# One transfer for both image halves, stores by column half, an earlier branch, and a projection that writes PSUM in image order

## The chip, the cores and the metric

The kernel runs on 1 core of one Trainium2 chip. The metric is device time in microseconds of that core. Everything is float32. TensorE (PE) multiplies and writes PSUM, VectorE (DVE) and ScalarE (ACT) read PSUM and SBUF, GpSimd (POOL) works on SBUF and issues transfers, SyncE (SP) only issues transfers. Transfers issued by SP and ACT go through the hardware queues, those issued by POOL through the software queue; all of them are carried out by the core's 16 DMA engines.

## What is computed

The input is one image x of 48 channels and 256x256 pixels. Two layers follow one another:

```
# layer 0
qkv = einsum('bchw,oc->bohw', gn(x), w_qkv)            # 144 channels
qkv = depthwise 3x3 convolution of qkv
q, k, v = heads(unfold 4x4 patches, 8 heads)           # 96 values x 64*64 patches (+ a border) per head
attn = softmax(l2norm(q)^T l2norm(k) * temperature)    # 4096 x 4096 per head
x = x + einsum('bchw,oc->bohw', fold(v attn), w_proj)
# layer 1, on windows of 64x64
x = x + sum over t of 3: einsum('bcphqw,twW,thH,tcC->bCpHqW', gn(x), Ws, Hs, Cs)
```

`gn` is a group normalisation over 16 groups of 3 channels, so each layer begins only when the statistics of its whole input are known.

## The kernel before

The image's 256 rows are kept as two halves of 128 rows: channel c of half s lies on partition 16 + 48 s + c, so that 96 partitions are filled. `rows_of[s]` names the 48 partitions of half s. `both_halves` and `both_parts` return a list with one piece of DRAM for each half, and every caller loops over that list and issues one transfer of 48 partitions for each half.

The stages, in order of time:

1. **Load and statistics** (L427 to L445). x is read into `xr` (112 partitions, 128 rows of 256) in ten parts, two transfers each, all on SP's queue. DVE takes `bn_stats` of each part as it arrives; then `group_stats` gives mean and deviation and everything that follows on PE depends on it.
2. **1x1 convolution of the first two heads** (L491 to L519). Sixteen steps. In each, PE multiplies into PSUM, ACT and DVE move the result to one of four tiles `oi`, and four transfers (column half `c` times image half `s`, half of them on SP, half on POOL) store it to `t1[0]` in DRAM. The `oi` tiles are in the same pool as `xr`.
3. **Depthwise convolution of head 0** (`depthwise_first`). Ten rows of patches: `Depthwise.load` reads `pad` from `t1` in three transfers, the taps run on PE (matrices `diag`, made on POOL at L387) or on DVE, and three stores write queries, keys and values to `qkv[0]`.
4. **A branch** (L538). If the temperatures are large, another path computes row maxima. With these inputs it is not taken, but every engine loads the flag, compares and passes a series of semaphore events.
5. **Attention** (L572 to L801), one head after the other, in an order written out by hand (`tc.manual_schedule`). Sixteen steps g per head. The depthwise convolution of head h+1 runs beside head h. During head 0 also the 1x1 convolution of heads 2 to 7 runs, in 32 `Strip`s: `load` reads 4 rows of both halves into one of two tiles `xs` (two transfers on SP), `run` multiplies, `store` writes to `t1[1]` (two transfers on SP). On SP's queue the load of strip j+2 stands behind the store of strip j. During head 7 the rows of x for three parts of the projection are loaded into `xts` (L799).
6. **Projection** (`project`, L809 to L902). The image is cut into 8 parts of 32 rows, 16 in each half. For each, PE multiplies the attention's output (`pot0` or `pot`, in patch order) by `w_proj`, DVE adds the result to x in place and takes the statistics for layer 1, and POOL stores the rows to `x1s`. For parts 3 to 7 the rows of x are loaded on SP's queue at L894, behind the loads of `pot`. PSUM holds a patch order (kj, py, px), and DVE reads and writes with a step of four elements when it adds.
7. **Layer 1** (L930 to L1083). Pieces of x1 in SBUF and rows read back from `x1s` go through three products; the output is stored from POOL.

The lines of the projection and of the strip load that matter:

```
for half, rows in enumerate(both_parts(x1s, k, part * R, R)):          # L829
    nc.gpsimd.dma_start(out=rows, in_=xt[rows_of[half]])
for s, rows in enumerate(both_parts(xc, k, part * R, R)):              # L893
    nc.sync.dma_start(out=xt[rows_of[s]], in_=rows)
```

Of the kernel before, what the change touches and what calls it, by code (L numbers as in the profile page):

```python
# [19 lines left out]
HALF = H // 2  # L20
# [29 lines left out]
def conv_preact_kernel(  # L50
# [73 lines left out]
    for z in range(3):  # L124
        for j in range(CH):
            p = (z * CH + j) * 6
            nc.gpsimd.dma_start(out=dwt[p : p + 6], in_=dws[z])
    nmx = const.tile([128, NH * NT // 128], F32, name="nmx")
    nc.vector.memset(nmx, 0.0)
# [34 lines left out]

    def both_halves(t, y, n, base=0):

        return [t[:, base + s * HALF + y : base + s * HALF + y + n, :] for s in range(2)]

    order = [(3, 0), (3, 1), (2, 0), (2, 1), (1, 1), (1, 0), (0, 1), (0, 0)]

    def both_parts(t, k, y, n):

        yw, i = order[k]
        y += yw * WS + i * TP // PX * KS
        return [t[:, y + s * (WS // 2) : y + s * (WS // 2) + n, :] for s in range(2)]

    class Strip:
# [5 lines left out]
        def load(self):  # L183
            self.xs = xss[self.j % len(xss)]
            for s, rows in enumerate(both_halves(xc, SR * self.j, SR)):
                nc.sync.dma_start(out=self.xs[rows_of[s]], in_=rows)

# [20 lines left out]
        def store(self):  # L208
            for s, rows in enumerate(both_halves(t1[1], SR * self.j, SR, base=1)):
                nc.sync.dma_start(out=rows, in_=self.ot[:, s])  # L210
# [171 lines left out]
    def depthwise_first():  # L382

        with tc.tile_pool(name="dg", bufs=1) as dg, tc.tile_pool(name="dps", bufs=3, space=PSUM) as dps:
            diag = dg.tile([NP1, 9, NP1], F32, name="diag")
            for t in range(9):
                nc.gpsimd.tensor_scalar_mul(diag[:, t, :], ident[:NP1, :NP1], dwt[:, 0, t : t + 1])  # L387
# [3 lines left out]
            def taps(r):  # L391
# [12 lines left out]
            with tc.manual_schedule(engines={mybir.EngineType.PE}):  # L404
                taps(0)
                for i in range(0, CR + 1, 2):
                    if i + 1 not in on_tensor:
                        taps(i + 1)
                    taps(min(i + 2, CR))
                    for d in rows[i + 6 : i + 8]:  # L410
# [15 lines left out]

    with tc.tile_pool(name="xn", bufs=1) as xnp, tc.tile_pool(name="cst", bufs=1) as cst, tc.tile_pool(  # L427
        name="nps", bufs=2, space=PSUM
    ) as nps, tc.tile_pool(name="pw", bufs=3, space=PSUM) as pw:
# [8 lines left out]
        for i, LR in enumerate(parts):  # L438
            j = sum(parts[:i])
            clear(xr[:, j : j + LR, :])  # L440
            for s, rows in enumerate(both_halves(xc, j, LR)):
                nc.sync.dma_start(out=xr[rows_of[s], j : j + LR, :], in_=rows)
            for i in range(0, LR, 2):
                nc.vector.bn_stats(st0[:, (j + i) // 2, :], xr[:, j + i : j + i + 2, :].rearrange("p a b -> p (a b)"))
# [47 lines left out]
        QR = HALF // 2  # L492
        ois = [xnp.tile([128, 2, OR, W + 2], F32, name=f"oi{i}") for i in range(4)]
        for t in ois:
            nc.gpsimd.memset(t[:, :, :, 0:1], 0.0)
            nc.gpsimd.memset(t[:, :, :, W + 1 : W + 2], 0.0)
        for n in range(QR // OR):
# [19 lines left out]
            for c in range(2):  # L517
                for s, rows in enumerate(both_halves(t1[0], c * QR + n * OR, OR, base=1)):
                    (nc.gpsimd if s else nc.sync).dma_start(out=rows, in_=ot[c * 64 : c * 64 + M0, s])  # L519

# [13 lines left out]
    for t in xss:  # L534
        nc.gpsimd.memset(t[:OFF], 0.0)
    depthwise_first()

    with tc.If(nc.values_load(large) > 0):  # L538
        with tc.tile_pool(name="sps", bufs=2, space=PSUM) as sps:
            for j in range(HALF // SR):  # L540
# [3 lines left out]
                w.store()  # L544
        for h in range(1, NH):
            depthwise_all(h)
        with tc.tile_pool(name="mk", bufs=NM) as mk, tc.tile_pool(name="mq", bufs=2) as mq, tc.tile_pool(
            name="mps", bufs=2, space=PSUM
        ) as mps:
            for h in range(NH):  # L550
# [5 lines left out]
                for nb in range(NB):  # L556
# [12 lines left out]
                    b = h * NB + nb  # L569
                    nc.vector.tensor_reduce(nmx[:, b : b + 1], mx, AX.X, ALU.max, negate=True)  # L570

    with tc.tile_pool(name="ahead", bufs=2) as ah, tc.tile_pool(name="ae", bufs=3) as ae, tc.tile_pool(  # L572
# [128 lines left out]
        with tc.manual_schedule():  # L701
            load_query(0, 1)
            block = scores(0, 0)
            for h in range(NH):
                more = h + 1 < NH
                rows = {r: Depthwise(h + 1, r) for r in range(CR + 1)} if more else {}
                for g in range(NG):
# [68 lines left out]
                    for k in range(NK):  # L776
# [18 lines left out]
                        if not more and 0 < g <= 2 * NX and k in (1, 3):  # L795
                            i = (g - 1) * 2 + k // 2
                            t, y = i // 4, i % 4 * (RP // 4)
                            for half, src in enumerate(both_parts(xc, t, y, RP // 4)):
                                nc.sync.dma_start(out=xts[t][rows_of[half], y : y + RP // 4, :], in_=src)  # L799
                        if not more and 2 * NX < g <= 2 * NX + KS and k in (1, 3):  # L800
# [8 lines left out]
        def project(k, pot, part, xt, new):  # L809

            R = xt.shape[1]
            n = R // KS * PX
            xv = xt.rearrange("p (py ki) (px kj) -> p ki kj py px", ki=KS, kj=KS)
            for ki in range(KS):
                ps = new(n)
                step = 512 // n
                for i in range(0, KS, step):
                    nc.tensor.matmul(  # L818
                        ps[:, i : i + step, :],
                        lhsT=wp,  # L820
                        rhs=pot(ki)[:PF, i : i + step, part * n : (part + 1) * n],
                        start=True,
                        stop=True,
                    )
                nc.vector.tensor_add(xv[:, ki], ps.rearrange("p k (py px) -> p k py px", py=R // KS), xv[:, ki])
            for i in range(0, R, 2):
                nc.vector.bn_stats(st1[:, len(seen), :], xt[:, i : i + 2, :].rearrange("p a b -> p (a b)"))
                seen.append(i)
            for half, rows in enumerate(both_parts(x1s, k, part * R, R)):  # L829
                nc.gpsimd.dma_start(out=rows, in_=xt[rows_of[half]])  # L830

        def in_big(n):

            ps = big.tile([128, 2, 512], F32, name="big")
            return ps[:PF].rearrange("p a (b n) -> p (a b) n", n=n)

# [24 lines left out]

    with tc.tile_pool(name="pj", bufs=1) as pj, tc.tile_pool(name="pjs", bufs=1) as pjs, tc.tile_pool(
        name="pps", bufs=3, space=PSUM
    ) as pps, tc.tile_pool(name="pp1", bufs=1, space=PSUM) as pp1:
# [21 lines left out]
        for k, xus_k in enumerate(xus, 1):  # L886
# [3 lines left out]
            if k >= NX:  # L890
                for part, xt in enumerate(xus_k):
                    R = xt.shape[1]
                    for s, rows in enumerate(both_parts(xc, k, part * R, R)):  # L893
                        nc.sync.dma_start(out=xt[rows_of[s]], in_=rows)  # L894
            for part, xt in enumerate(xus_k):
# [4 lines left out]
                    xt,  # L900
                    lambda n: pps.tile([PF, KS, n], F32, name="pps"),
                )  # L902
# [222 lines left out]
```

## Time and profile before

| what | value |
|---|---|
| median of 3 runs | 3569.47 us (3565.06 to 3577.12) |
| the profiled execution | 3563.74 us, its span 3561.9 us |
| mean granted TensorE clock | 0.978 |
| PE busy | 3324.8 us, 93% of the span |
| DVE, ACT, POOL busy | 1982.3, 1953.2, 588.0 us |
| HBM read, written | 230.82 MB, 144.90 MB |

The span runs from the first to the last instruction; the profiled execution's own time is 1.8 us longer. By stage, read from the order of the instructions: x is loaded and its statistics taken until 88 us; the first 1x1 convolution runs to 150 us; the depthwise convolution of head 0 from 158 to 277 us; the first product of the attention begins at 291 us; head 0 lasts to about 745 us and the attention to 3188 us; the projection begins at 3196 us, layer 1 at 3325 us. A share of busy time is an average over stages that have different limits, so each stage must be looked at by itself.

### The profile page before, as it was taken

The page shows a single profiled execution, that of the slowest core. Times are in us where ns is not written, and L with a number is a line of the kernel's source. Part 1 is how long each engine was busy: PE and PEld are TensorE (multiplying, and loading weights), DVE is VectorE, ACT ScalarE, POOL GpSimd, SP SyncE. Part 2 cuts the span into 40 slices and gives each one's busy share as a digit, 9 for nine tenths or more (in the row PEclk, how much of TensorE's full clock was granted, in tenths as well). Part 3 has the DMA queues.
Part 4 walks back from the last instruction along what each step waited for, and adds up shares of the span by engine and source line. Part 5 has one row for each costly group of instructions (what it writes and reads, how often), then busy time and mean ns, then how long its engine had stood idle before and what let it go on. Part 6 is the DMA issues. An engine that isn't in the chain of part 4 may idle for free.

```text
span 3561.9 us, 63455 instructions
## 1 busy us (share of the span) xinstructions
PE 3324.8 (93%) x25964; PEld 1856.3 (52%) x25964; DVE 1982.3 (56%) x2965; ACT 1953.2 (55%) x2891; POOL 588.0 (17%) x658
## 2 busy tenths in 40 slices
PE   0696999999999999999999999999999999986898
PEld 0243445555555555555555555555555555542576
DVE  4372666148825882588258826872687222228544
ACT  3234667657755665566557655764666444423243
POOL 2231111012211220122012201220122010000123
PEclk9897999999999999999999999999999999997999
DMA  9445666543332333333333332333333222109764
GB/s 147 143 127 147 164 161 165 168 137 93 86 87 79 93 87 83 89 95 82 85 87 95 79 87 83 93 89 78 87 96 93 76 53 51 33 25 295 176 163 112
DMA packets 232563, 380.22 MB, mean 107 GB/s; under 512 B 77858, under 2 KB 176546, under 8 KB 229192
## 3 DMA queue, kind: packets, MB, share of 16 engines
q1 hardware_dynamic: 192246, 262.98, 27.6%
q0 software_dynamic: 36544, 110.12, 13.7%
q8 instruction: 208, 3.41, 0.4%
q10 hardware_dynamic: 3474, 2.97, 0.3%
q14 instruction: 91, 0.75, 0.1%
HBM read 230.82 MB, written 144.90 MB: 105 GB/s over the span
## 4 chain that ended last, share of the span: by engine, by line
PE 85%; DMA 5%; DVE 1%; issue 1%; SPq 0%; ACT 0%; POOL 0%; POOLq 0%; DVEq 0%; ACTq 0%
PE big L361 39%; PE big L651 36%; PE pb L1015 2%; PE pa L991 2%; PE pc L1034 2%; DMA lxq<-in_x_dram 2%; PE big L194 2%; DMA xs<-in_x_dram 2%; PE pst L599 1%; DMA kt<-qkv 0%; PE pn L268 0%; PE pps L818 0%; DVE acc L249 0%; PE big L818 0%; DMA pad<-t 0%
## 5 line engine op out<-in xcount | busy, mean ns | idle before, releaser
L617 ACT ACTIVATE e<-big,nmx 128x1024 f32<-128x1024 f32 x1024 | 1144.6, 1118 | 909.6 <-PE big L361 883.7
L361 PE MATMUL big<-kt,qt 128*128 128x512 f32 x6144 | 1459.9, 395 | 29.7 <-DMA qt<-qkv 23.4
L651 PE MATMUL big<-e,vn 128*32 128x512 f32 x12288 | 1348.4, 593 | 1.0 <-DVE vn L635 1.0
L361 PEld LDWEIGHTS big<-kt,qt 128*128 128x128 f32 x6144 | 1143.3, 189 | 370.0 <-issue 122.0
L665 DVE TENSOR_TENSOR oacc<-big,oacc 128x1024 f32<-128x1024 f32 x359 | 438.5, 1221 | 766.9 <-PE big L651 766.9
L651 PEld LDWEIGHTS big<-e,vn 128*32 128x32 f32 x12288 | 384.5, 110 | 881.9 <-issue 815.5
L249 DVE SCALAR_TENSOR_TENSOR acc<-pad,dwt,acc 126x1024 f32<-126x1024 f32 x592 | 765.5, 1293 | 34.0 <-ACT acc L230 18.3
L319 POOL DMA_DIRECT2D qkv<-o x72 | 52.9, 734 | 1341.0 <-ACT o L303 1341.0
L313 POOL TENSOR_TENSOR ol<-o,oh 126x1024 fp32r<-126x1024 f32 x78 | 185.3, 2376 | 266.5 <-DVE ss L264 197.4
L631 DVE TENSOR_REDUCE zt<-zs 128x1 f32<-128x5 f32 x256 | 38.6, 151 | 327.6 <-ACT e L617 291.2
L617 ACT ACTIVATION_READ_ACCUMULATOR e<-big,nmx 128x1 f32 x1024 | 195.8, 191 | 0.0
L303 ACT COPY o<-acc 126x1024 f32<-126x1024 f32 x74 | 161.8, 2186 | 0.0
L1022 ACT COPY lyt<-pb 128x1024 f32<-128x1024 f32 x69 | 69.9, 1012 | 111.6 <-PE pb L1015 111.6
L201 ACT ACTIVATE ot<-big,bias 108x1024 f32<-108x1024 f32 x64 | 68.0, 1112 | 112.2 <-PE big L194 74.9
L230 ACT ACTIVATE acc<-pad,dwt 126x1024 f32<-126x1024 f32 x74 | 84.1, 1136 | 77.8 <-DMA pad<-t 69.7
L676 POOL DMA_DIRECT2D os__70<-oacc x86 | 50.3, 593 | 424.2 <-DVE oacc L665 414.4
L238 PE MATMUL dps<-pad,diag 126*126 126x512 f32 x216 | 95.6, 602 | 19.3 <-DMA pad<-t 19.3
L260 ACT ACTIVATE sq<-acc 126x1024 f32<-126x1024 f32 x74 | 78.2, 1057 | 59.6 <-DVE acc L249 48.5
L335 POOL DMA_DIRECT2D kt<-qkv x44 | 22.9, 538 | 516.6 <-PE big L361 418.9
L818 PE MATMUL pps<-pot,wp 112*112 112x512 f32 x112 | 68.9, 775 | 39.0 <-DMA pot<-os__70 20.7
L1001 DVE COPY lzt<-pa 128x864 f32<-128x864 f32 (+1 forms) x69 | 67.5, 1000 | 59.9 <-PE pa L991 59.9
L264 DVE TENSOR_REDUCE ss<-sq 126x64 f32<-126x1024 f32 x80 | 97.3, 1218 | 5.4 <-ACT sq L260 5.3
(154 smaller groups left out, 1973.4 us busy)
## 6 DMA issues: line engine op xcount, KB each, us to landing
pad<-t SPq DMA_DIRECT2D x238, 254.0 KB
t<-ot SPq DMA_DIRECT2D x64, 435.4 KB
qkv<-ol POOLq DMA_DIRECT2D x78, 336.0 KB, 6.4
qkv<-oh POOLq DMA_DIRECT2D x70, 336.0 KB, 5.7
qt<-qkv SPq DMA_DIRECT2D x176, 96.0 KB
xs<-in_x_dram SPq DMA_DIRECT2D x64, 192.0 KB
out_dram<-lrt POOLq DMA_DIRECT2D x96, 128.0 KB, 3.5
qkv<-o POOLq DMA_DIRECT2D x72, 168.0 KB, 3.4
```

What stands on the lines that cost most here:

```text
L194: nc.tensor.matmul(ps[:M1, s, :], lhsT=wr[r], rhs=self.xs[r, i : i + 2, :].rearrange("p a b -> p (a b)"), start=True, stop=True,)
L230: nc.scalar.mul(self.acc, self.pad[:, 0:KS, 0:W], dwt[:, self.h, 0:1])
L238: nc.tensor.matmul(ps[:, i, :], lhsT=diag[:, tap, :], rhs=self.pad[:, y : y + 2, dx : dx + W], start=(tap == 0), stop=(tap == 8),)
L249: nc.vector.scalar_tensor_tensor(self.acc, self.pad[:, dy : dy + KS, dx : dx + W], dwt[:, self.h, tap : tap + 1], self.acc, ALU.mult, ALU.add,
L260: nc.scalar.activation(self.sq, self.acc, AF.Square)
L264: nc.vector.tensor_reduce(self.ss, self.sq.rearrange("p a (x b) -> p x a b", b=KS), AX.XY, ALU.add)
L303: nc.scalar.copy(self.o.rearrange("p (a b) x -> p a b x", a=KS), self.acc.rearrange("p a (x b) -> p a b x", b=KS))
L313: eng.tensor_sub(self.ol, self.o, self.oh.bitcast(F32))
L361: nc.tensor.matmul(ps[:, i, :], lhsT=qt[:, r, q0 : q0 + 128], rhs=kts[2 * j + i][:, r // 2, :], start=(r == 0), stop=(r == 2),)
L617: nc.scalar.activation(e[:, j * 1024 : (j + 1) * 1024], ps.rearrange("p a b -> p (a b)"), AF.Exp, bias=nmx[:, b : b + 1], accum_out=zs[:, ...
L651: nc.tensor.matmul(ps[p * 32 : (p + 1) * 32, u, :], lhsT=vn[:, c * 32 : (c + 1) * 32], rhs=e[:, n * 512 : (n + 1) * 512], start=(i == 0), ...
L665: nc.vector.tensor_add(oaccs[h, pair], ps, old)
```

## The change

- `both_halves` and `both_parts` return one view whose first dimension is the half (`s c y x`) instead of a list of two views. Six callers that looped over the halves now issue one transfer of 96 partitions: the load of `xr`, `Strip.load`, the loads of `xts` and of the projection's rows of x, and the store to `x1s`. `Strip.store` loops over the view's first dimension and issues two transfers as before.
- The first convolution stores by column half: one transfer for both image halves, `c` outermost, column half 0 from SP and 1 from POOL. The `oi` tiles are five, in a pool of their own.
- `diag` is made at the start of the kernel, in a pool of its own.
- The branch stands in front of `depthwise_first`; the path that is not taken computes head 0's convolution too.
- The projection's PSUM tiles have image order: PE writes them with a step of four elements, DVE reads and writes contiguous rows. `pxts` has a pool of its own.

```
@@ L125
+    taps = ExitStack()
+    diag = taps.enter_context(tc.tile_pool(name="diag", bufs=1)).tile([NP1, 9, NP1], F32, name="diag")
+    for t in range(9):
+        nc.gpsimd.tensor_scalar_mul(diag[:, t, :], ident[:NP1, :NP1], dwt[:, 0, t : t + 1])
@@ L165
-        return [t[:, base + s * HALF + y : base + s * HALF + y + n, :] for s in range(2)]
+        return t[:, : 2 * HALF, :].rearrange("c (s y) x -> s c y x", s=2)[:, :, y : y + n, :]
@@ L171
-        y += yw * WS + i * TP // PX * KS
-        return [t[:, y + s * (WS // 2) : y + s * (WS // 2) + n, :] for s in range(2)]
+        y += i * TP // PX * KS
+        return t.rearrange("c (w s y) x -> w s c y x", s=2, y=WS // 2)[yw, :, :, y : y + n, :]
@@ L183 Strip.load
-            for s, rows in enumerate(both_halves(xc, SR * self.j, SR)):
-                nc.sync.dma_start(out=self.xs[rows_of[s]], in_=rows)
+            nc.sync.dma_start(out=self.xs[OFF:], in_=both_halves(xc, SR * self.j, SR))
@@ L438
-            for s, rows in enumerate(both_halves(xc, j, LR)):
-                nc.sync.dma_start(out=xr[rows_of[s], j : j + LR, :], in_=rows)
+            nc.sync.dma_start(out=xr[OFF:, j : j + LR, :], in_=both_halves(xc, j, LR))
@@ L490
-        ois = [xnp.tile([128, 2, OR, W + 2], F32, name=f"oi{i}") for i in range(4)]
+        ois = [oip.tile([128, 2, OR, W + 2], F32, name=f"oi{i}") for i in range(5)]
@@ L517
-                for s, rows in enumerate(both_halves(t1[0], c * QR + n * OR, OR, base=1)):
-                    (nc.gpsimd if s else nc.sync).dma_start(out=rows, in_=ot[c * 64 : c * 64 + M0, s])
+                (nc.gpsimd if c else nc.sync).dma_start(
+                    out=both_halves(t1[0][:, 1:, :], c * QR + n * OR, OR).rearrange("s c y x -> c s y x"),
+                    in_=ot[c * 64 : c * 64 + M0],
+                )
@@ L536
-    depthwise_first()
-
     with tc.If(nc.values_load(large) > 0):
...
-        for h in range(1, NH):
+        for h in range(NH):
             depthwise_all(h)
...
+    depthwise_first()
+    taps.close()
@@ L798
-                            for half, src in enumerate(both_parts(xc, t, y, RP // 4)):
-                                nc.sync.dma_start(out=xts[t][rows_of[half], y : y + RP // 4, :], in_=src)
+                            nc.sync.dma_start(
+                                out=xts[t][OFF:, y : y + RP // 4, :], in_=both_parts(xc, t, y, RP // 4)
+                            )
@@ L809 project
-            n = R // KS * PX
-            xv = xt.rearrange("p (py ki) (px kj) -> p ki kj py px", ki=KS, kj=KS)
+            PY = R // KS
+            xv = xt.rearrange("p (py ki) x -> p ki py x", ki=KS)
             for ki in range(KS):
-                ps = new(n)
-                step = 512 // n
-                for i in range(0, KS, step):
+                ps = new(PY)
+                for y in range(0, PY, 2):
                     nc.tensor.matmul(
-                        ps[:, i : i + step, :],
+                        ps[:, y : y + 2, :].rearrange("p py (px kj) -> p kj py px", kj=KS),
                         lhsT=wp,
-                        rhs=pot(ki)[:PF, i : i + step, part * n : (part + 1) * n],
+                        rhs=pot(ki)[:PF, :, (part * PY + y) * PX : (part * PY + y + 2) * PX],
                         start=True,
                         stop=True,
                     )
-                nc.vector.tensor_add(xv[:, ki], ps.rearrange("p k (py px) -> p k py px", py=R // KS), xv[:, ki])
+                nc.vector.tensor_add(xv[:, ki], ps, xv[:, ki])
...
-            for half, rows in enumerate(both_parts(x1s, k, part * R, R)):
-                nc.gpsimd.dma_start(out=rows, in_=xt[rows_of[half]])
+            nc.gpsimd.dma_start(out=both_parts(x1s, k, part * R, R), in_=xt[OFF:])
@@ L866
-        pxts = [pj.tile([PF, r, W], F32, name=f"pxt{t}") for t, r in enumerate((RP, RP, PR))]
+        pxts = [pjx.tile([PF, r, W], F32, name=f"pxt{t}") for t, r in enumerate((RP, RP, PR))]
@@ L893
-                    for s, rows in enumerate(both_parts(xc, k, part * R, R)):
-                        nc.sync.dma_start(out=xt[rows_of[s]], in_=rows)
+                    nc.sync.dma_start(out=xt[OFF:], in_=both_parts(xc, k, part * R, R))
```

More of the change, by code (lines that the diff above doesn't have):

```diff
@@ L162, in group_stats, with both_halves @@
         nc.vector.reciprocal(rstd, g)
-    def both_halves(t, y, n, base=0):
-        return [t[:, base + s * HALF + y : base + s * HALF + y + n, :] for s in range(2)]
+    def both_halves(t, y, n):
+        return t[:, : 2 * HALF, :].rearrange("c (s y) x -> s c y x", s=2)[:, :, y : y + n, :]
     order = [(3, 0), (3, 1), (2, 0), (2, 1), (1, 1), (1, 0), (0, 1), (0, 0)]
@@ L208, in store @@
         def store(self):
-            for s, rows in enumerate(both_halves(t1[1], SR * self.j, SR, base=1)):
+            for s, rows in enumerate(both_halves(t1[1][:, 1:, :], SR * self.j, SR)):
                 nc.sync.dma_start(out=rows, in_=self.ot[:, s])
@@ L384, in depthwise_first, with on_row @@
         with tc.tile_pool(name="dg", bufs=1) as dg, tc.tile_pool(name="dps", bufs=3, space=PSUM) as dps:
-            diag = dg.tile([NP1, 9, NP1], F32, name="diag")
-            for t in range(9):
-                nc.gpsimd.tensor_scalar_mul(diag[:, t, :], ident[:NP1, :NP1], dwt[:, 0, t : t + 1])
             rows = [Depthwise(0, r, dg) for r in range(CR + 1)]
             on_tensor = [r for r in range(CR + 1) if r % 2 == 0 or r == CR]
-            def taps(r):
+            def on_row(r):
                 if r in on_tensor:
@@ L404, in depthwise_first @@
             with tc.manual_schedule(engines={mybir.EngineType.PE}):
-                taps(0)
+                on_row(0)
                 for i in range(0, CR + 1, 2):
                     if i + 1 not in on_tensor:
-                        taps(i + 1)
-                    taps(min(i + 2, CR))
+                        on_row(i + 1)
+                    on_row(min(i + 2, CR))
                     for d in rows[i + 6 : i + 8]:
@@ L427, in conv_preact_kernel @@
     with tc.tile_pool(name="xn", bufs=1) as xnp, tc.tile_pool(name="cst", bufs=1) as cst, tc.tile_pool(
+        name="oip", bufs=1
+    ) as oip, tc.tile_pool(
         name="nps", bufs=2, space=PSUM
@@ L828, in project @@
                 seen.append(i)
-            for half, rows in enumerate(both_parts(x1s, k, part * R, R)):
-                nc.gpsimd.dma_start(out=rows, in_=xt[rows_of[half]])
+            nc.gpsimd.dma_start(out=both_parts(x1s, k, part * R, R), in_=xt[OFF:])
         def in_big(n):
             ps = big.tile([128, 2, 512], F32, name="big")
-            return ps[:PF].rearrange("p a (b n) -> p (a b) n", n=n)
+            return ps[:PF].rearrange("p a (b x) -> p (a b) x", x=W)
         with tc.manual_schedule():
@@ L860, in load_piece @@
         eng.dma_start(out=piece(yw, i)[rows_of[s], y : y + n, :], in_=x1s[:, y0 : y0 + n, :])
-    with tc.tile_pool(name="pj", bufs=1) as pj, tc.tile_pool(name="pjs", bufs=1) as pjs, tc.tile_pool(
+    with tc.tile_pool(name="pjx", bufs=1) as pjx, tc.tile_pool(name="pj", bufs=1) as pj, tc.tile_pool(name="pjs", bufs=1) as pjs, tc.tile_pool(
         name="pps", bufs=3, space=PSUM
@@ L900, in conv_preact_kernel @@
                     xt,
-                    lambda n: pps.tile([PF, KS, n], F32, name="pps"),
+                    lambda n: pps.tile([PF, n, W], F32, name="pps"),
                 )
```

## The prediction

> **What bounds the kernel now.** I read first the page's chain of work that ended last, then the busy time by stretches, then the branch's line. The whole is PE's:
>
> ```profile
> span 3561.9 us, 63455 instructions
> PE 85%; DMA 5%; DVE 1%; issue 1%; SPq 0%; ACT 0%; POOL 0%; POOLq 0%; DVEq 0%; ACTq 0%
> ```
>
> The change touches none of the two attention products that make up most of PE's share. It touches transfers, and three stages that wait for them. Busy time by stretch (columns: stretch, length, busy time of PE, PEld, DVE, ACT, POOL, granted clock, DMA share, GB/s):
>
> ```profile
> 0.00:88.00 88.00, 0.00 (x0) 0.00 (x0) 41.97 (x89) 30.89 (x12) 23.32 (x54) 1.00 0.97 148
> ...
> 170.00:175.00 5.00, 5.00 (x12) 2.06 (x11) 3.11 (x3) 1.15 (x1) 0.00 (x0) 0.96 0.45 170
> 190.00:195.00 5.00, 5.00 (x13) 2.16 (x12) 4.86 (x5) 0.00 (x0) 0.00 (x0) 1.00 0.45 178
> 345.00:745.00 400.00, 389.84 (x2440) 202.41 (x2440) 212.08 (x329) 263.29 (x373) 57.19 (x52) 0.98 0.62 167
> 3210.00:3310.00 100.00, 67.19 (x110) 24.08 (x110) 82.99 (x87) 23.81 (x6) 7.51 (x15) 0.77 1.00 290
> ```
>
> The load of x (first line) has all 16 DMA engines busy and no PE. Head 0 (fourth) has PE at 97% and DMA at 62%. The projection (last) has the DMA engines full again. Lines two and three are the key: only `pad` loads run there, at a share of 0.45, which is 7.2 of 16 engines, however many wait behind. The `pad` view in DRAM has a first dimension of 7, while 42 partitions stand on the other side.
>
> The branch, by its source line on SP:
>
> ```profile
> L538 SPq EVENT_SEMAPHORE  x8: 17/17/17, 285.1 to 285.7; - x8
> L538 SPq TENSOR_LOAD <-large x1: 982/982/982, 281.2 to 281.2; - x1
> L538 SPq COMPARE_BRANCH  x1: 50/50/50, 282.2 to 282.2; - x1
> ```
>
> SP reaches it last, after head 0's stores; its first attention load is issued at 286.3, and POOL and ACT wait for SP's events.
>
> **What the Trainium skill says.** "DMA: Bandwidth & Descriptors", section "Why a DMA increments its semaphore by 16 and not by 1": a transfer runs on the largest k up to 16 that divides the slowest dimension of both sides, as the instruction carries it. The 7 busy engines of `pad` (7 against 42) agree. The same section says that hardware-queue transfers take the lowest-numbered k engines, software-queue ones k consecutive engines that rotate; no line here shows either. "PSUM — Partial Sum Buffer", "Specifications (TRN2)": a non-contiguous pattern slows matmuls significantly, with no figure; all matmuls of before write contiguously, so the trace is silent.
>
> **The change part by part.** The new view is (s=2, c=48, y, x) against 96 partitions. The largest divisor of both 2 and 96 is 2: **each merged transfer runs on two engines.** One engine moves 170/7 to 178/7 GB/s in the `pad` lines, 24.3 to 25.4; I take 25, so a pair moves 50 GB/s.
>
> *Load of x.* 2 x 48 x 128 KB = 12.58 MB, by 50 GB/s 252 us, and the first packet some 2 us after the start: 254 us, against about 88 x 0.97 = 85 us and a last `bn_stats` at 88. Nothing hides it, since everything waits for the statistics. **+165** (155 to 175 from 25.4 and 24.3 GB/s, less a microsecond or two). The ten DMA issues saved on SP (0.31 us each) are hidden. `diag`, nine POOL instructions of 0.6 us, moves from 160 us to behind the `dwt` loads at 81 us; the load covers it, and without that cover it costs its 5.3 us. On POOL only the `zr` memset and the zero rows' stores stand behind it.
>
> *First convolution.* 36 channels stay outermost and 12 divides 36, so the engines stay as they were. 64 stores become 32 of twice the size, and a fifth buffer eases ACT's 21.6 us and DVE's 13.8 us of waits for `t<-oi`. The traffic, 64 x 145 KB = 9.3 MB over 12 x 25 GB/s, needs 31 us of the 50 us that the stores take, so at most some 15 us could go; bigger transfers could also hold a buffer longer. **-5** (-12 to +3).
>
> *The branch.* Moved ahead, it stands between the last `t1[0]` stores and the `pad` loads of SP and ACT. SP needs 281.2 to 286.3, 5.1 us, for it; now it waits there from 153.6 to 158.35, 4.7 us, for the stores to land, which covers the new place to within half a microsecond. POOL's memsets and DVE's next work wait for the same stores. Without that cover it costs 5 us. At the old place 5.1 us go, but the key loads then wait for head 0's last stores, issued until 281.1 and landing after a POOL-like median of 6.4 us. The first query and strip loads, needing older rows only, can be early; PE's idle time from 269.3 to 291.2 is the limit. **-5** (-15 to +4).
>
> *Head 0's strips.* 32 loads of 393 KB, 15.7 us per pair at a whole-step pace of two per 26.4 us. Over the 400 us line, an average engine is busy 0.62 x 400 = 248 us. Without the strips' 11.4 MB (28 us per engine) 220 are left. The two lowest engines carry more: 7.0 MB of `pad` on 7 engines is 40 us instead of 17; 26 MB of `t<-ot` on 12 (108 channels) is 87 instead of 65. That gives 265 us, and with strips on two engines, 11.4 MB/50 = 228, **493 us in a stretch of 400**. If bytes alone count (167 GB/s, so 167 us instead of 248), it is 412. So DMA takes over from PE as the bound of head 0: +12 to +93 at perfect overlap, more if SP's queue stalls behind the pair. I take **+90** (10 to 190). `Strip.store` is unchanged; 32 saved issues are hidden. *Head 7's* 12 merged loads (7.9 us each, two per 22 us) can delay query loads: **+2** (0 to 6).
>
> *Projection.* x for parts 3 to 7 is 7.86 MB: 157 us on the pair, from SP's first issue at 3207. In the same queue stand five `pot` loads, a sixteenth of 1.57 MB per engine each, 5 x 3.9 = 20 us; one rotating x1s store of 1.57 MB on the same pair would add some 20. The last x lands between 3384 and 3404; now it lands at 3302.9. **+85** (60 to 130). DVE's adds get cheaper (2024 ns to about the 1221 of `oacc`'s contiguous add, same size), about 24 us in all, hidden behind the loads. PE's stepped writes cost from nothing (below is excluded: the same columns stream) to a doubling of 775 ns; only the first part's 16 x 795 ns lie ahead of the first load: **+3** (0 to 13). The last x1s store takes 15.7 us instead of 5.5 before layer 1 reads it: **+3** (0 to 10), covered by the first products. `pjx` only moves addresses: nothing, covered by the load in front of any new wait.
>
> Sum: 165 - 5 - 5 + 90 + 2 + 85 + 3 + 3 = **+338**. The profiled execution took 3563.7 us, so 3902; it lies 6 us under the median: **3908 us**. All low ends give 3768, all high ends 4101.
>
> **Rivals.** *Hidden strips.* PE stays head 0's bound, because contention falls when only two engines are heavily loaded. For: the byte count gives 412 of 400. Against: waits for `xs` exist already. 3908 - 90 = 3818. *Blocked queue.* SP issues in order; a full pair holds query and `pad` loads too, and an `xs` issue already takes up to 3.9 us where the median is 0.6. Twice the stall: about 4000. *No confinement*, the other side: the view is carried with the channels outermost, or spread after all, over 16 engines. Then the load stays at 148 GB/s, which decides from about 6 engines (6 x 25) upward; the gains of stores (-5), branch (-5) and adds (10 of 24, since DMA is at 1.00) less 3 for PE remain, 3569 - 17 = 3552. Against it stand the two 0.45 lines; for it, that reordering 7 x 6 would not have shown.
>
> **How the numbers follow.** Pair-bound strips, 3908: 0.57. Hidden strips: 0.20. Blocked queue: 0.15. No confinement: 0.07. Anything else, near 3569: 0.01. The range 3780 to 4040 takes in the first three without their far ends. About 0.3% (11 us) is what a measurement can tell from no change: faster 0.07, same 0.01, slower 0.92.
>
> **What would show it.** The first 250 us at a DMA share near 0.13 and 50 GB/s, last `bn_stats` near 255 instead of 88; head 0 near 545 us (now 291 to 745) with PE waiting for `xs`; the first `pa` product some 85 us later after the last attention product than now (137 us); adds at L825 near 1.2 us. A DMA share near 1 in the load would refute the confinement, and with it the sum; PE at 97% in head 0 would leave 3818.

## The result, and the profile after

The changed kernel takes **3932.19 us** (median, 3925.77 to 3937.62) where the kernel before, run beside it, takes 3567.26 us (3563.75 to 3577.12): 365 us more, a ratio of 1.1017, 95% interval 1.0989 to 1.1046. The prediction was 3908 us, range 3780 to 4040. The profiled execution of the changed kernel took 3933.79 us, its span is 3932.0 us and the mean granted clock 0.955.

The chain of work that ended last, page of the changed kernel: shares of the span by engine, then by line.

```profile
PE 73%; DMA 10%; another core or an unknown queue 3%; DVE 2%; SPq 2%; issue 1%; ACT 1%; POOL 0%; POOLq 0%; DVEq 0%; ACTq 0%
PE big L364 34%; PE big L655 30%; DMA xs<-in_x_dram 7%; PE pb L1017 2%; PE pa L993 2%; PE dps L241 2%; PE pc L1036 2%; SPq L338 1%; PE big L197 1%; DVE st L831 1%; DMA pxt<-in_x_dram 1%; DMA kt<-qkv 0%; SPq L229 0%; PE pst L603 0%
```

PE's share fell from 85% to 73%. The loads of the strips (`xs`) grew from 2% of the chain to 7%, some 275 us. The chain cannot be followed back beyond 315 us, so the load of x is not in it, and 3% of it have no name: in the projection they stand where DVE waits for loads of x. Busy time by stretch of the changed kernel, with the columns of the prediction's table (stretch, length, PE, PEld, DVE, ACT, POOL, granted clock, DMA share, GB/s): the load of x, head 0, the projection.

```profile
0.00:240.00 240.00, 0.00 (x0) 0.00 (x0) 41.28 (x87) 30.89 (x12) 28.71 (x65) 1.00 0.14 54
470.00:1010.00 540.00, 447.05 (x2642) 231.09 (x2642) 222.78 (x347) 288.36 (x412) 58.96 (x56) 0.90 0.45 133
3480.00:3690.00 210.00, 73.46 (x126) 26.84 (x125) 71.83 (x104) 14.93 (x5) 6.52 (x9) 0.64 0.38 130
```

The load of x moves 54 GB/s at a DMA share of 0.14, where it was 148 GB/s at 0.97. The projection was at a share of 1.00 and is at 0.38. The DMA engines as a whole are not short of time; most of them are idle while everything waits. The groups show who waits (busy us, mean ns, then the idle time of the engine and what ended it), first before, then in the changed kernel:

```profile
L818 PE MATMUL pps<-pot,wp 112*112 112x512 f32 x112 | 68.9, 775 | 39.0 <-DMA pot<-os__70 20.7 <-DVE pxt L825 8.5 <-DVE lxq L825 5.5
L194 PE MATMUL big<-xs,wr 64*108 64x512 f32 (+1 forms) x256 | 68.9, 626 | 10.2 <-DMA xs<-in_x_dram 10.1
L444 DVE BATCH_NORM_STATS2 st<-xr 112x6 f32<-112x512 f32 x64 | 38.6, 676 | 34.2 <-DMA xr<-in_x_dram 34.2
```

```profile
L822 PE MATMUL pps<-pot,wp 112*112 112x512 f32 x112 | 69.0, 775 | 137.3 <-DVE lxq L829 70.8
L197 PE MATMUL big<-xs,wr 64*108 64x512 f32 (+1 forms) x256 | 83.0, 776 | 89.1 <-DMA xs<-in_x_dram 89.1
L445 DVE BATCH_NORM_STATS2 st<-xr 112x6 f32<-112x512 f32 x64 | 39.0, 679 | 193.8 <-DMA xr<-in_x_dram 193.8
```

`bn_stats` waits 193.8 us for x (34.2 us before), the strip products 89.1 us for `xs` (10.1 us before). The projection's products wait for DVE, and the adds on DVE wait in turn for the loads (changed kernel; us in total, times, longest):

```profile
DVE lxq L829 <- DMA lxq<-in_x_dram: 71.3, 4, 34.5
DVE pxt L829 <- DMA pxt<-in_x_dram: 36.8, 2, 22.4
```

By stage, from the ends and starts of the instructions that bound each (`oacc` collects the attention's output of a head, `pa` is the first product of layer 1):

| stage | before | after | difference |
|---|---|---|---|
| start to last `bn_stats` | 88.2 | 242.2 | +154.0 |
| to the last copy of the first convolution | 60.8 | 59.1 | -1.7 |
| to the first depthwise product | 17.9 | 22.9 | +5.0 |
| depthwise products of head 0 | 99.6 | 99.7 | +0.1 |
| to the first attention product | 24.7 | 33.9 | +9.2 |
| to the first copy into `oacc` | 36.8 | 31.7 | -5.1 |
| head 0, to head 1's first copy | 433.5 | 540.6 | +107.1 |
| heads 1 to 7, to the last attention product | 2426.2 | 2426.2 | 0.0 |
| to the first `pa` product (projection) | 136.9 | 234.7 | +97.8 |
| layer 1 | 237.3 | 241.0 | +3.7 |

The differences add up to 370.1 us, the difference of the two spans. Each figure is of one execution. The kernels of the experiments below, taken where they share a stage with the kernel before, spread by some microseconds: 85.1 to 93.0 us to the last `bn_stats`, 58.8 to 62.2 for the first convolution with either kind of stores, 237.0 to 246.3 for layer 1. So the -1.7 and the +3.7 of the table can't be told from nothing.

### The profile page after: what moved, and what is told of

It reads as the page before. It is cut to its first block, busy times and chain, and to the rows that moved or that the text cites. A ratio compares the mean times of both kernels' runs of the same rounds, so it can differ in the third digit from the quotient of the medians.

```text
span 3932.0 us, 63314 instructions
## 1 busy us (share of the span) xinstructions
PE 3345.3 (85%) x25964; PEld 1862.7 (47%) x25964; DVE 1959.1 (50%) x2965; ACT 1953.2 (50%) x2891; POOL 578.9 (15%) x634
## 4 chain that ended last, share of the span: by engine, by line
PE 73%; DMA 10%; another core or an unknown queue 3%; DVE 2%; SPq 2%; issue 1%; ACT 1%; POOL 0%; POOLq 0%; DVEq 0%; ACTq 0%
PE big L364 34%; PE big L655 30%; DMA xs<-in_x_dram 7%; PE pb L1017 2%; PE pa L993 2%; PE dps L241 2%; PE pc L1036 2%; SPq L338 1%; PE big L197 1%; DVE st L831 1%; DMA pxt<-in_x_dram 1%; DMA kt<-qkv 0%; SPq L229 0%; PE pst L603 0%
## 5 line engine op out<-in xcount | busy, mean ns | idle before, releaser
L197 PE MATMUL big<-xs,wr 64*108 64x512 f32 (+1 forms) x256 | 83.0, 776 | 89.1 <-DMA xs<-in_x_dram 89.1
L445 DVE BATCH_NORM_STATS2 st<-xr 112x6 f32<-112x512 f32 x64 | 39.0, 679 | 193.8 <-DMA xr<-in_x_dram 193.8
L241 PE MATMUL dps<-pad,diag 126*126 126x512 f32 x216 | 96.9, 609 | 25.4 <-DMA pad<-t 25.4
```

Of the source, the lines that this page charges most:

```text
L197: nc.tensor.matmul(ps[:M1, s, :], lhsT=wr[r], rhs=self.xs[r, i : i + 2, :].rearrange("p a b -> p (a b)"), start=True, stop=True,)
L241: nc.tensor.matmul(ps[:, i, :], lhsT=diag[:, tap, :], rhs=self.pad[:, y : y + 2, dx : dx + W], start=(tap == 0), stop=(tap == 8),)
```

## The experiments

The theory is the prediction's: a merged transfer runs on two DMA engines, and the stages that wait for such transfers carry the loss. The rivals: the other edits carry part of it; the merging itself is slow, not the number of engines; or the stages depend on each other, so that the loss can't be assigned to one of them. Each run was made beside the kernel before; differences are taken to the median of before in the same group (3566.83, 3563.48 or 3568.67 us).

**Two transfers again, all else kept (`e1_two_transfers`).** The same cut at all five kinds of transfer whose merged view has the half outermost; the one of the strips:

```
-            nc.sync.dma_start(out=self.xs[OFF:], in_=both_halves(xc, SR * self.j, SR))
+            for s in range(2):
+                nc.sync.dma_start(out=self.xs[rows_of[s]], in_=both_halves(xc, SR * self.j, SR)[s])
```

> The changed kernel with each of its five merged transfers (load of x, strips, the projection's two kinds of x loads, the stores of x1s) cut into one transfer per half again; all other edits stay. If the pairs of DMA engines are the whole cause (theory), nothing but the small edits is left: 3552 us by the prediction's sum without confinement, within 3535 to 3570. If the other edits carry part of the loss (rival: the branch at its new place, the stores by column half or the stepped PSUM writes), it stays above 3580. If the gap of 25.4 us between first convolution and first depthwise product comes from the branch's new place, it stays near 25 us here; if it was late DMA work of the pair, it returns to 19.

Measured: 3555.36 us, ratio 0.9972 (0.9961 to 0.9983). The whole loss is in the merged transfers, and what is left of the change is a gain of 11.5 us, close to the 17 us that the prediction gave the edits if nothing were confined, though not from the edits that it named (below). The first two of the groups above, in this kernel:

```profile
L823 PE MATMUL pps<-pot,wp 112*112 112x512 f32 x112 | 64.3, 726 | 35.4 <-DMA pot<-os__70 16.6 <-DVE pxt L830 10.9 <-DVE lxq L830 3.8
L198 PE MATMUL big<-xs,wr 48*108 48x512 f32 (+1 forms) x256 | 66.1, 614 | 4.7 <-DMA xs<-in_x_dram 4.7
```

The wait for `xs` is 4.7 us where it was 89.1. The gap ahead of the first depthwise product is 20.6 us, counted from the last copy of the first convolution; before it was 17.9, in the changed kernel 22.9. That does not yet tell whether the branch holds it: in the twelve kernels with the branch at its old place the same gap is 15.2 to 19.4 us, one execution each. (The expectation's 25.4 and 19 us count from the last product, 22.0 here, and 21.9 in `e4`, which has the branch at its old place.)

**One merged site at a time.** Four kernels, each the kernel before with one kind of transfer merged. The edit of the first, and of the others likewise:

```
-            for s, rows in enumerate(both_halves(xc, j, LR)):
-                nc.sync.dma_start(out=xr[rows_of[s], j : j + LR, :], in_=rows)
+            nc.sync.dma_start(out=xr[OFF:, j : j + LR, :], in_=merged_halves(xc, j, LR))
```

`e2_x_load_merged`, the load of x alone:

> The kernel before with only the load of x merged. Theory, two engines: last bn_stats near 242 us as in the changed kernel, DMA share 0.14, and the whole +154 us, 3721 us, since nothing later depends on it. Rival, that the pace of the load was set by something else in the changed kernel (the diag products moved ahead on POOL, the changed order of DMA issues): the last bn_stats returns to about 88 us and the time to 3567.

Measured: 3714.10 us, ratio 1.0415 (1.0384 to 1.0446), +147 us. The last `bn_stats` ends at 241.9 us. Busy time of a stretch in the middle of this load, with nothing else under way:

```profile
120.00:140.00 20.00, 0.00 (x0) 0.00 (x0) 4.85 (x8) 0.00 (x0) 0.00 (x0) 1.00 0.13 54
```

A share of 0.13 of 16 engines is 2.1 engines, and 54 GB/s is 27 GB/s for each. No view names the engines. No more engines join although transfers wait: at 120 us SP has issued six of the ten (the sixth by 107.5 us) and three have landed (the fourth part's `bn_stats` begin at 122.9). So the transfers of this queue share one pair.

`e3_strips_merged`, head 0's strips alone (`Strip.load`):

> The kernel before with only head 0's strip loads merged. Theory, the DMA engines become head 0's bound because two of them carry all the strips: head 0 takes the changed kernel's 541 us between first output copies instead of 433, time 3567 + 107 = 3674 us. Rival, hidden strips (the stall comes from the branch and the late query loads ahead of it): under 3600. Rival, that part of the 107 us is a backlog from before head 0: between 3620 and 3660.

Measured: 3677.01 us, ratio 1.0294 (1.0261 to 1.0328), +110 us. Head 0 takes 534.8 us. Its strip group, and then its stretch of head 0:

```profile
L203 PE MATMUL big<-xs,wr 64*108 64x512 f32 (+1 forms) x256 | 81.6, 764 | 83.3 <-DMA xs<-in_x_dram 83.3
```

```profile
340.00:850.00 510.00, 420.84 (x2506) 215.79 (x2504) 219.14 (x339) 272.32 (x384) 59.05 (x56) 0.91 0.46 136
```

PE is busy 83% of a stretch that it filled to 97%, and it waits for `xs` as in the changed kernel, although neither the branch nor the load of x differs from before. So neither an earlier backlog nor late query loads are needed for it.

`e4_proj_loads_merged`, the projection's x loads alone (`xts` in head 7 and parts 3 to 7):

> The kernel before with only the projection's x loads merged (head 7's twelve and parts 3 to 7), its stores of x1s still two per part. If the loads on one pair set the pace (theory), 7.86 MB at 50 GB/s: the stretch from the last attention product to the first pa product grows from 137 us to 215 to 235, time 3645 to 3665 us. If it is the stores of x1s that held the buffers (rival), the stretch stays under 170 and the time under 3600.

Measured: 3682.78 us, ratio 1.0322 (1.0292 to 1.0352), +116 us. The stretch from the last attention product to the first `pa` product is 256.9 us, more than the expected 235 and more than the 234.7 of the changed kernel. Who waited for the loads, in this stretch (us in total, times, longest):

```profile
DVE pxt L836 <- DMA pxt<-in_x_dram: 68.2, 3, 29.4
DVE lxq L836 <- DMA lxq<-in_x_dram: 62.9, 4, 28.8
```

The loads set the pace, but a bare 157 us for their bytes is too little. In this kernel the first add into `pxt` comes 85.6 us after the last attention product; in the changed kernel it comes after 66.2 us, which is nearly all of the 22 us between them. Other edits of the change can account for it: the merged stores, and an earlier `pot` with the image order (below), with which the same add comes after 43.4 us in `e12`, against 58.0 before. No run combines any of them alone with the merged loads, so their parts stay open.

`e5_proj_stores_merged`, the stores of x1s alone:

> The kernel before with only the projection's x1s stores merged, one transfer per part on POOL's queue. The loads merged alone cost 116 us where the changed kernel's whole projection lost 98, so the merged stores do not add to it. Theory: each store runs on another pair of engines, off the loads' way, and only the last one is late for layer 1: 0 to +6 us, 3567 to 3573. Rival: all of them stand on one pair, 12.58 MB at 50 GB/s = 252 us from the first part on, so layer 1 waits: above 3650.

Measured: 3594.45 us, ratio 1.0091 (1.0060 to 1.0121), +31 us. Both expectations missed. The last `bn_stats` ends at 3320.3 us, some 11 us later after the last attention product than before, and the first `pa` product follows 27.3 us later, where 7.1 was enough before. What that product waited for, from the chain that ended last (start us, us, what):

```profile
3291.91 45.97 DMA x1s<-pxt
...
3338.18 0.69 ACTq L946
...
3344.72 0.21 ACT gsg L161
...
3347.58 3.28 PE pa L1000 x24
```

One store of x1 that reads `pxt`, the seventh of ten, is issued at 3291.9 us and lands 46.0 us later. ACT's queue is held until then at L946, the load of a weight of layer 1 into `wsb`. Behind it in ACT's order stands `gsg`, a step of layer 1's statistics, and without it no `pa` product can start. That `wsb` lies where `pxt` lay is an inference; the chain shows the wait. So about 20 us of the 31 are this wait, and the other 11 lie ahead of the last `bn_stats`. All ten stores land late: 26.5 to 94.0 us after issue, median 58.9 (before: 4.1 to 19.7, median 13.5). In the changed kernel no such wait shows: the last store that reads `pxt` lands at 3669.8 us, but the x loads end so late that the last `bn_stats` ends only at 3685.3, and the first `pa` product comes 5.7 us after it.

The four sites cost 147 + 110 + 116 + 31 = 404 us one by one, the other edits give 11.5 back, which makes 393; the change costs 365. The missing 28 us agree in size with the stores' 31, of which the late loads cover at least the wait. This is an agreement in size and no full account: the stretch with the loads alone (`e4`) is also 22 us longer than the changed kernel's.

**Is it the number of engines, or the merging? (`e9_46_and_2`)** Nothing is merged here; each half's 48 channels go as 46 and 2.

```
             for s, rows in enumerate(both_halves(xc, j, LR)):
-                nc.sync.dma_start(out=xr[rows_of[s], j : j + LR, :], in_=rows)
+                o = rows_of[s].start
+                for a, b in ((0, 46), (46, 48)):
+                    nc.sync.dma_start(out=xr[o + a : o + b, j : j + LR, :], in_=rows[a:b])
```

> The kernel before with the load of x in four transfers per step instead of two: nothing merged, but the 48 channels of each half go as 46 and 2. Theory, the number of engines is the largest divisor up to 16 of the slowest dimensions: 46 has 2, so these too run on two engines, the last bn_stats near 242 us and the time near 3714, as with the load merged. Rival, it is the merging itself (a view of two strided halves in one transfer) that is slow: 46 channels go as fast as 48, last bn_stats at 88 to 95, time 3565 to 3575.

Measured: 3722.94 us, ratio 1.0437 (1.0403 to 1.0470); the last `bn_stats` ends at 241.9 us, the very time of the merged load. Its stretch:

```profile
80.00:120.00 40.00, 0.00 (x0) 0.00 (x0) 4.85 (x8) 0.00 (x0) 0.00 (x0) 1.00 0.13 54
```

Again 2 of 16 engines and 54 GB/s, with four times as many transfers. The merging is not what is slow; the divisor decides, as the Trainium skill says ("DMA: Bandwidth & Descriptors", section "Why a DMA increments its semaphore by 16 and not by 1"). This was tested on the load of x; for the strips, the projection's loads and the stores, where other transfers run beside them, the same cause is carried over.

**Another queue (`e10_merged_on_pool`).**

```
-            nc.sync.dma_start(out=xr[OFF:, j : j + LR, :], in_=merged_halves(xc, j, LR))
+            nc.gpsimd.dma_start(out=xr[OFF:, j : j + LR, :], in_=merged_halves(xc, j, LR))
```

> The kernel before with the load of x merged as in the change, but issued on POOL's queue in place of SP's. Theory, a software queue gives each transfer another pair of engines: the ten transfers run beside each other, a 1.57 MB transfer takes at least 31 us, and the last bn_stats comes at 88 to 125 us, time 3565 to 3605. Rival, every merged transfer stands on the same pair whatever its queue: 242 us and 3714.

Measured: 3667.88 us, ratio 1.0287 (1.0241 to 1.0332); the last `bn_stats` ends at 185.8 us, between the two expectations. Busy time of a stretch in which only this load runs, then the load's line (issues: shortest, median and longest ns, first and last start; below, who is waited for, and the time to landing):

```profile
40.00:80.00 40.00, 0.00 (x0) 0.00 (x0) 0.00 (x0) 0.00 (x0) 0.00 (x0) 1.00 0.51 92
```

```profile
L451 POOL DMA_DIRECT2D xr<-in_x_dram x10: 720/738/757, 21.6 to 97.1; - x10
its engine sat idle before it (us, times) until:
  DMA xr<-in_x_dram: 66.8, 2
...
DMA to landing us min/median/max: 68.9/76.8/80.6
```

About 8 engines are busy (0.51 x 16), and in this stretch just four of the ten transfers are under way (issued from 21.6 to 26.7 us, the next at 90.7): two engines for each, and another pair for each, which agrees with what the same section of the skill says of software queues. But the load starts at 21.6 us, behind 20 us of other issues on POOL, the fifth issue waits 64 us for earlier transfers of the load itself, and the 8 engines move only 92 GB/s, 11 GB/s each. Later, from 100 to 120 us, with the other six issued, the share is 0.90 and the rate still 96 GB/s. Moving the merged load to POOL regains 48 us of the 147, no more.

**The small edits one by one.** `e6_branch_behind` is the kernel with two transfers and all small edits, with the branch and the end of the `diag` pool put back behind the convolution:

```
+    depthwise_first()
+    taps.close()
     with tc.If(nc.values_load(large) > 0):
...
-    depthwise_first()
-    taps.close()
```

> The kernel with two transfers everywhere and all other edits of the change (3555 us), with the branch and the diag pool's closing back behind the convolution. It separates the branch's new place from the other edits. By the prediction the new place gains 5 us, so this one would take 3560. Rival, read from the traces: the new place costs 2.7 us ahead of the first depthwise product (20.6 us from the last copy of the first convolution to the first depthwise product, against 17.9 before) and gains 2.2 us behind it: within 3552 to 3558, no difference. A third, that it costs 5 us at the new place and gains nothing: 3550.

Measured: 3550.76 us, ratio 0.9957 (0.9940 to 0.9973), against 0.9972 (0.9961 to 0.9983) with the branch in front: the intervals overlap, the branch's place can't be told from no difference. By stage it seems to cost in front (20.6 us to the first depthwise product in `e1`, 15.2 here) and to gain behind (22.5 us to the first attention product, 24.5 here): the eleven other kernels with the branch at its old place have 16.4 to 19.4 and 23.2 to 24.9.

`e7_image_order` is the kernel before with only the projection's PSUM in image order (the change's edit of `project`):

```
-                nc.vector.tensor_add(xv[:, ki], ps.rearrange("p k (py px) -> p k py px", py=R // KS), xv[:, ki])
+                nc.vector.tensor_add(xv[:, ki], ps, xv[:, ki])
```

> The kernel before with only the projection's PSUM in image order: PE's stepped writes and DVE's contiguous adds. Prediction: adds 2010 to about 1215 ns, 10 us of their 24 reach the end, less up to 3 for PE: 3560. Theory after the traces: PE's products stay at 775 ns and the stretch from the last attention product to the first pa product goes from 137 to 129 us: 3559. Rival, the adds are hidden behind the x loads (DMA share 1.00 there): 3567, no change.

Measured: 3560.60 us, ratio 0.9996 (0.9983 to 1.0010): no difference. The adds went from 2015 to 1210 ns, but the stretch to the first `pa` product is 138.8 us (136.9 before): the rival was right, the loads cover the adds.

`e8_stores_by_column` is the kernel before with only the first convolution's stores by column half and five `oi` tiles in a pool of their own:

```
-                for s, rows in enumerate(both_halves(t1[0], c * QR + n * OR, OR, base=1)):
-                    (nc.gpsimd if s else nc.sync).dma_start(out=rows, in_=ot[c * 64 : c * 64 + M0, s])
+                (nc.gpsimd if c else nc.sync).dma_start(
+                    out=merged_halves(t1[0][:, 1:, :], c * QR + n * OR, OR).rearrange("s c y x -> c s y x"),
+                    in_=ot[c * 64 : c * 64 + M0],
+                )
```

> The kernel before with only the first convolution's stores by column half, in a pool of their own with five buffers. Prediction: -5 us, with -12 to +3 open. The two traces give 54.5 us from first to last product of that convolution before, 51.6 in the changed kernel and 54.6 in the one with two transfers and the same stores, so theory now: nothing, 3567. Rival: bigger stores land later, the pad loads start later, up to +3.

Measured: 3560.90 us, ratio 0.9995 (0.9980 to 1.0010): no difference. These stores are also merged over the halves, but with the channels outermost, and they cost nothing.

So far nothing explains the gain of the small edits. What is left is the pool. `e11_own_pool` is the kernel before with it alone:

```
-        pxts = [pj.tile([PF, r, W], F32, name=f"pxt{t}") for t, r in enumerate((RP, RP, PR))]
+        pxts = [pjx.tile([PF, r, W], F32, name=f"pxt{t}") for t, r in enumerate((RP, RP, PR))]
```

> The kernel before with only the pxt tiles in a pool of their own. Prediction: the pool only moves addresses, nothing: 3565. Theory after the traces of the kernel with two transfers: the pot tiles no longer lie where the first part's operands do, ACT's clears of pot start 0.2 instead of 18 us after the last attention product, and the stretch to the first pa product shrinks from 137 us to 128 to 132: 3558 to 3561.

Measured: 3557.29 us, ratio 0.9975 (0.9964 to 0.9986), 11.4 us faster; the stretch to the first `pa` product is 129.6 us. ACT's groups just after the last attention product, first before, then with the pool of its own (the idle time, and what ended it, stand last):

```profile
L120 ACT COPY pot<-plain 16x4096 f32<-16x4096 f32 x3 | 10.6, 3599 | 28.4 <-PE big L818 28.4
```

```profile
L120 ACT COPY pot<-plain 16x4096 f32<-16x4096 f32 x3 | 10.7, 3600 | 10.9 <-PE big L651 10.5 <-DMA kt<-os__70 0.4
```

Before, the clears of `pot` wait for L818, the products of the projection's first part; with the pool they wait for L651, the last attention product, and start 0.1 us after it instead of 18.0. The loads of `pot` that follow on SP begin 6.5 us after it instead of 18.0, beside the first part and not behind it. The stretch to the first `pa` product is 136.1 to 138.8 us in the seven kernels that have neither the pool nor merged transfers in the projection, and 122.7 to 129.6 in the four that have the pool and no merged transfers.

`e12_order_and_pool` joins the two edits of the projection, and nothing else of the change:

> The kernel before with two of the change's edits: PSUM in image order and the pool of the pxt tiles, nothing else. If these two are all that is of use in the change (theory): the stretch from the last attention product to the first pa product 125 to 130 us as with all small edits, 3553 to 3557, ratio 0.997. If each alone gives nothing and the gain of the kernel with two transfers came from the stores or the branch (rival): 3563 to 3567.

Measured: 3553.18 us, ratio 0.9966 (0.9952 to 0.9979); the stretch to the first `pa` product is 122.7 us, shorter than expected. The interval lies below that of the image order alone (`e7`) and overlaps those of the three other kernels with the pool and without merged transfers (`e1`, `e6`, `e11`). So the pool gains, and what the stores, the branch and the image order add to it these runs can't tell. For the image order this is close: its median is 4.1 us below that of the pool alone, and the first add into `pxt` comes 43.4 to 44.2 us after the last attention product in the three kernels that have both, after 54.2 with the pool alone and 52.6 with the image order alone. Once `pot` comes early, cheaper adds may count; more runs of these two kernels would have to show it.

## Why the prediction held, and where its terms were off

The mechanism and the sign held. The two engines, the pace of a pair, head 0 turning from PE's to the DMA engines' stage and the late projection are all in the traces. The sum was +338 on the profiled execution and the spans differ by 370; these 32 us, term by term (in part luck: the terms are 45 us too small and 13 us too large together, and two, the load of x and the branch, lie outside their own ranges):

| term | predicted | measured |
|---|---|---|
| load of x | +165 | +154 |
| first convolution | -5 | -1.7 |
| branch | -5 | +9 (+5.0 +9.2 -5.1) |
| head 0 | +90 | +107 |
| head 7's loads | +2 | 0 |
| projection, stepped writes with it | +85 +3 | +98 |
| last store, before layer 1 | +3 | +3.7 |

**Load of x.** The pair moved 54 GB/s, not the 50 taken from the `pad` lines: 12.58 MB / 54 is 233 us and not 252. `e2` gives +147 for it alone. The low end of the range, 155, is wider than its working, which gives about 160 at 25.4 GB/s; the measured 154 lies below both.

**First convolution.** Within its range; `e8` shows no worth of the edit alone. ACT and DVE wait there 26.9 us for stores of `oi` instead of 35.4, and the time stays the same: these waits did not set it.

**The branch.** This term had the wrong sign. "Covers the new place to within half a microsecond" failed. The branch by its line in the changed kernel (issues or times in ns, first and last start):

```profile
L539 SPq EVENT_SEMAPHORE  x8: 17/17/17, 309.3 to 311.1; - x8
...
L539 SPq COMPARE_BRANCH  x1: 45/45/45, 302.6 to 302.6; - x1
...
L539 POOLq TENSOR_LOAD <-large x1: 503/503/503, 311.5 to 311.5; - x1
```

SP compares at 302.6 and then waits with its events until 311.1; the last store that POOL issued lands at 310.9. Only then does POOL load the flag, and the `pad` loads are issued at 315.1, 13.8 us after the last copy of the first convolution, where 9.4 were enough before. The stores' landing and the branch stand one behind the other, not beside each other. At the old place 5.1 us go, but the gain is 2.2 us in `e1`, and it turns into a loss of 9.2 in the changed kernel, where PE stands idle 31.0 us before the first attention product (21.9 before) and SP needs 15.8 us to issue the first six query loads, against 4.1 in `e1`. In `e3`, with the branch behind, the merged strip loads are issued only after the first keys, and this stage takes 24.5 us. That strip loads, now free to start earlier, stand ahead of the keys on the pair is an inference; no run has the merged strips with the branch in front and nothing else.

**Head 0.** The working gave 493 us on the two lowest engines in a stretch of 400, +93 at perfect overlap; +90 was chosen and +107 came. It is not the wait that was taken too small. Head 0 from first copy to first copy, before and in the changed kernel, with the same number of PE's products:

```profile
328.00:761.50 433.50, 423.34 (x2636) 221.09 (x2632) 222.25 (x345) 285.02 (x405) 59.52 (x56) 0.98 0.61 165
489.50:1030.10 540.60, 447.22 (x2636) 229.33 (x2632) 222.22 (x345) 286.31 (x405) 59.46 (x56) 0.90 0.45 132
```

PE stands idle 93.4 us instead of 10.2, which is 83 more, and the other 24 us are products that take longer, at a granted clock of 0.90 instead of 0.98. `e3` shows the same (445 us busy at 0.91), `e1` and `e2`, which do not wait, have 419 and 421 us busy at 1.00 and 0.99. The prediction put this at nothing; why less clock is granted in a stage that waits no run here shows. `e3` has 534.8 us of head 0 where the kernels with unmerged strips have 424 to 439. The hidden-strips rival, PE at 97%, is refuted by PE's 83%; the blocked queue (twice the stall) did not come.

**Projection.** Right in kind, 13 us too small without the stepped writes. The bare bytes at 50 GB/s gave the floor, and what else stands on the pair was put at 20 us; `e4` shows 116 us for the loads alone.

**Last store.** The +3 took the last x1s store for the one that counts, and agrees with +3.7 by chance, since layer 1 spreads by more. `e5` shows that merged stores alone cost 31 us, 20 of them through an earlier store that holds ACT's queue; the late loads hide it.

**Stepped PSUM writes.** Nothing. The projection's products before and in the changed kernel (shortest, median and longest ns):

```profile
L818 PE MATMUL pps<-pot,wp x112: 592/593/1195, 3215.5 to 3312.8; 112*112 112x512 f32 x112
L822 PE MATMUL pps<-pot,wp x112: 592/592/1196, 3477.2 to 3681.1; 112*112 112x512 f32 x112
```

As the ends of products are modelled, their pace counts too: four in a row take 1.97 us before and 1.97 us in `e7`. The page "PSUM — Partial Sum Buffer" ("Specifications (TRN2)") says that a non-contiguous pattern slows matmuls significantly; for this pattern, 512 float32 columns written at a step of 4, no such cost shows.

**The pool `pjx`.** "Only moves addresses: nothing" was wrong, and it is the one edit that gains: 11.4 us alone, inside a loss of 365. Where a tile lies can decide which earlier instruction its first write waits for: here the clear of `pot` waited for L818, and with the pool for L651. For the adds the prediction let 10 of 24 us reach the end in its last rival; alone none did (`e7`).

**No confinement.** The rival's time, 3552, is close to what `e1` gave, 3555, but by luck: its 17 us were stores, branch and adds, of which no run shows a gain, and the pool, with 11.4 us, stood in it as nothing. Its point of decision, six engines, was too low: `e10` has eight busy and 92 GB/s, on the other queue.

## What to carry to other kernels

Before two transfers are merged, write down the outermost dimension of both sides as the instruction will carry it; a view (2, 48, ...) against 96 partitions leaves two engines working, and DMA share times 16 in a stretch with one kind of transfer shows it at once. Merge with the long dimension outermost (as the stores by column half do) or not at all: in `e8` 32 saved issues beside other work gained nothing. No run here merges the loads with the channels outermost. When tiles change pools, look at what the first write of each waits for: here the only edit that gained by itself let a clear start without waiting for another part's products, and in `e5` a weight's load waited for a store.

## What the runs showed that was not expected

- For the same load of x, a pair of engines moves 27 GB/s for each, eight engines 11 GB/s (92 / 8.2, on POOL's queue), all sixteen 9.5 GB/s (148 / 15.5). So the rate grows far less than the number of engines, and a share near 1 does not mean that each engine moves what it can. What holds them is open. The Trainium skill ("DMA: Bandwidth & Descriptors", "Latency and other measured facts") reports slower copies where rows of DRAM lie a large power of two apart; the channels of x lie 256 KB apart, a pitch for which it has no figure, and no run here changes it.
- Head 0 took 424 to 439 us, one profiled execution each, in the twelve kernels with unmerged strip loads (the same strip and attention code), and it is the largest difference between them outside the edits. Single spans 10 us apart prove nothing for this kernel; the stretch that holds the edit, and ratios over many runs, do.
- The merged stores of x1s, one of which holds up layer 1 through ACT's queue, cost 31 us alone and nothing visible beside the late loads. A cost measured alone need not be there in the sum.
